# Ending a layer in two halves of rows, and beginning the next layer's sums with the first half

## The chip, the cores and the metric

The kernel runs on one core of one Trainium2 chip. The metric is the device time of one execution in microseconds, from start to end on that core. The core has a matrix engine (TensorE, "PE" in the profile), a vector engine (VectorE, "DVE"), an activation engine (ScalarE, "ACT"), a general engine (GpSimd, "POOL") and a queue engine (SyncE, "SP") that here issues most of the DMA transfers. All inputs are in HBM; the host only transposes adj and three weight matrices beforehand.

## The reference

A graph has N = 2708 nodes with D = 128 features and a dense adjacency matrix adj (2708 x 2708, about 2.4% of it nonzero). Four layers follow each other, each wrapped in the same residual normalization:

```python
x = _layernorm(x + L0(x, adj))      # gelu messages of all pairs, weighted by adj; update, gelu, layer norm
x = _layernorm(x + L1(x, adj))      # messages gated by sigmoid(q k^T) * adj * adj; update, relu, layer norm
x = _layernorm(x + L2(x, adj))      # hyperbolic attention over all pairs, expmap/logmap, relu
x = _layernorm(x + L3(x, adj))      # two sums over neighbours:

def L3(x, adj):
    neigh1 = adj @ x
    x1 = swish(neigh1 @ W + b)
    neigh2 = adj @ x1
    return swish(neigh2 @ W + b)
```

Each row of a layer's result needs every row of the input, since adj is dense in layout: `adj @ x` sums over all nodes. The sum itself may be taken in any order of nodes.

## The kernel before, in words

The 2708 rows lie in 22 row tiles of 128 rows (NT = 22, the last one has 20). x stays in SBUF as a tile of 128 partitions x 22 x 128. `runs()` cuts the row tiles into two halves, 0 to 10 and 11 to 21, and HT = 11 is the same cut.

**The order of the work.** A scheduler orders the instructions of each engine in most of the program; inside `tc.manual_schedule()` they stay in the order in which they are written. Engines take their instructions in that order, one after the other, and wait for each other by semaphores. Every DMA of adj tiles is issued by SP, in order as well.

**The ends of layers 0 and 1.** The class `Resnorm` does a layer norm of the layer's result h, the multiplication by its weight, the addition to x, and the layer norm of the sum. `normalize` takes the row moments of a run of tiles (`st`), makes a scale and an offset per row from them by a dozen small DVE instructions and one square root on ACT, and then shifts tile after tile, the even ones on DVE and the odd ones on ACT. `add(a, b)` normalizes h, multiplies and adds for a whole half at once, and takes the moments of x; `end(a, b)` normalizes x. In layer 0 the order is: add of the early half, the update of the last row tiles (`U.sums`, `U.rows`), add of the late half, end of the early half, end of the late half, then a few small operations that count rows with a problem (`bad`, `bad_n`). In layer 1 `Resnorm.all()` does the same without anything in between. Layer 1 begins with transposes of x and products with it, in groups of four row tiles; layer 2 begins with transposes of x and the products M.

**Layer 2's end.** The generator `end(hf)` does a half of the rows: transposes, then elementwise work in steps, with a `yield` after each. DVE works over 11 row tiles in each step, by `each` (one instruction per row tile), by `total` (a reduction) or by a chain of `Values` on 128 x 11 elements; ACT squares, takes square roots, tanh and logarithms. The last step normalizes x. A loop takes a step of end(1) (tiles 11 to 21), a step of end(0), and so on in turns:

```python
ends = [end(1), end(0)]
while ends:
    for e in list(ends):
        try:
            next(e)
```

**Layer 3.** `neighbours` keeps the whole transposed sum (128 x 2708) in six PSUM banks and adds adj tile after adj tile to it: for row tile j, x[:, j, :] is the stationary operand and the j-th 128 rows of adjT (1354 KB) stream past it, in six matmuls of up to 512 columns. HELD = 10 of the 22 adj tiles (0 to 9) are fetched ahead and kept for both passes; the other twelve come through three buffers in SBUF (STREAM = 3), whose pool is opened after the memory of layer 2's end is given back. `in_turns` mixes kept ("h") and streamed ("f") tiles. The second pass takes x1, made of the first pass's sums, in the same way, and after it rows are normalized and written out.

Of the kernel before, what the change touches and what calls it, by code (L numbers as in the profile page):

```python
# [20 lines left out]
P = 128  # L21
# [18 lines left out]
def gnn_stack(ctx: ExitStack, tc: tile.TileContext, t, out: bass.AP):  # L40
# [26 lines left out]
    @functools.cache  # L67
    def across(name):
        n = t[name].shape[0]
        r = const.tile([P, n], F32, name=f"row_{name}")  # L70
        nc.gpsimd.dma_start(out=r, in_=t[name].partition_broadcast(P))
        return r

# [27 lines left out]
    class Values:  # L101
# [33 lines left out]
        def add(self, a, b):  # L135
            return self.tt(a, b, ALU.add)
# [61 lines left out]

    def normalize(dst, src, st, a, b, V, sq=None):

        even, odd, m2, m5 = (st[:, a:b, k] for k in (1, 4, 2, 5))

        def stt(in0, scalar, in1, op0, op1):
            o = V.new(in0)
            nc.vector.scalar_tensor_tensor(o, in0, scalar, in1, op0=op0, op1=op1)
            return o


        d = V.tt(even, odd, ALU.subtract)
        q = stt(d, 1.0 / 16.0, d, ALU.mult, ALU.mult)  # L210
        if sq is None:
            m = stt(m2, LN_EPS * D, m5, ALU.add, ALU.add)
            w = stt(m, 0.25 / D, q, ALU.mult, ALU.add)
        else:
            m = V.tt(m2, m5, ALU.add)
            var = stt(m, 0.25 / D, q, ALU.mult, ALU.add)
            w = V.ts(var, 0.25 * LN_EPS, ALU.add)

        root = V.act(w, AF.Sqrt)
        both = V.tt(even, odd, ALU.add)  # L220
        r = V.recip(V.add(root, V.mul(w, V.recip(root))))
        off = stt(both, -0.5, r, ALU.mult, ALU.mult)
        if sq is not None:
            nc.vector.scalar_tensor_tensor(sq[:, a:b], var, 4.0 * D, V.mul(r, r), op0=ALU.mult, op1=ALU.mult)
        for i in range(a, b):
            c = slice(i - a, i - a + 1)
            if i % 2:
                nc.scalar.activation(dst[:, i, :], src[:, i, :], AF.Identity, bias=off[:, c], scale=r[:, c])  # L228
            else:
                nc.vector.tensor_scalar(dst[:, i, :], src[:, i, :], r[:, c], off[:, c], op0=ALU.mult, op1=ALU.add)  # L230

    class Resnorm:
# [4 lines left out]

        def add(self, a, b):
            h = self.h
            normalize(h, h, self.st, a, b, self.V)  # L240
            nc.vector.tensor_tensor(h[:, a:b, :], h[:, a:b, :], over_tiles(self.g, b - a), op=ALU.mult)
            nc.vector.tensor_tensor(x[:, a:b, :], self.xb[:, a:b, :], h[:, a:b, :], op=ALU.add)
            moments(self.st2, x, a, b)

        def end(self, a, b):
            normalize(x, x, self.st2, a, b, self.V, self.sq)

        def all(self):
            for a, b in runs():
                self.add(a, b)  # L250
            for a, b in runs():
                self.end(a, b)
# [124 lines left out]
    with ExitStack() as l0:  # L377
# [10 lines left out]
        with ExitStack() as msg:  # L388
# [449 lines left out]
            with tc.manual_schedule():  # L838
# [46 lines left out]
                early, late = runs()  # L885
                U.norm.add(*early)
                for n in range(ahead, G):
                    U.sums(n)
                for n in range(ahead, G):
                    U.rows(n)  # L890
                U.norm.add(*late)
                U.norm.end(*early)
                U.norm.end(*late)

# [10 lines left out]
                ps = p_misc.tile([P, BANK // P, P], F32, name="ps")  # L905
                nc.tensor.matmul(ps[:1, 0, :1], ones, most, start=True, stop=True)
                nc.vector.tensor_copy(bad_n, ps[:1, 0, :1])
# [68 lines left out]
    def layers_1_to_3(top, before_end=lambda: None):  # L976

        with ExitStack() as l1:
# [9 lines left out]
            w_both = wp.tile([P, 2 * D], F32, name="w_both")  # L988
            b_both = wp.tile([P, 2 * D], F32, name="b_both")
            xb = wp.tile([P, NT, D], F32, name="xb")  # L990
            w_msg, w_q, w_k = weight("L1_gnn_W_msg"), weight("L1_gnn_W_q"), weight("L1_gnn_W_k")
            upd_x, upd_a = weight("L1_gnn_W_upd", 0), weight("L1_gnn_W_upd", P)
            msg_bc, msg_br = column("L1_gnn_b_msg"), across("L1_gnn_b_msg")
            gate_b = across("L1_gnn_gate_bias")
            upd_b, gamma, beta = across("L1_gnn_b_upd"), across("L1_gnn_ln_gamma"), across("L1_gnn_ln_beta")

            with ExitStack() as pre:
                psum = pre.enter_context(tc.tile_pool(name="ps_pre1", bufs=2, space=PSUM))
                nc.gpsimd.memset(both[:, NT - 1, :], 0.0)
                for k, (w, b) in enumerate(((w_msg, msg_br), (upd_x, upd_b))):  # L1000
                    nc.gpsimd.tensor_copy(w_both[:, k * D:(k + 1) * D], w)
                    nc.gpsimd.tensor_copy(b_both[:, k * D:(k + 1) * D], b)
# [418 lines left out]
        HELD = min(NT, 10)  # L1421
        held = top.enter_context(tc.tile_pool(name="adj3", bufs=1))
        kept = {}
# [4 lines left out]
        with ExitStack() as fin:  # L1428
            fp = fin.enter_context(tc.tile_pool(name="fin2", bufs=1))
            tp = fin.enter_context(tc.tile_pool(name="fin2t", bufs=2))  # L1430
            psum = fin.enter_context(tc.tile_pool(name="ps_fin2", bufs=6, space=PSUM))
            VT0 = fp.tile([P, HW], F32, name="VT0")
            nc.sync.dma_start(out=VT0, in_=v_tab)
            for j in range(HELD):
                kept[j] = held.tile([P, N], F32, name=f"held{j}")
                nc.sync.dma_start(out=kept[j], in_=adjT[j * P:(j + 1) * P, :])
            u = fp.tile([P, NT, D], F32, name="u")
            sv = fp.tile([P, NT, D], F32, name="sv")
            st = fp.tile([P, NT, 6], F32, name="st")
            nc.gpsimd.memset(u[:, NT - 1, :], 0.0)  # L1440
            nc.gpsimd.memset(V0, 0.0)

            def end(hf):
                a, b = ((0, HT), (HT, NT))[hf]
                n = b - a
                V = Values(fp, f"v2{hf}_")
# [4 lines left out]
                def temp():  # L1451
                    return tp.tile([P, max(HT, NT - HT), D], F32, name="tmp")[:, :n, :]
# [76 lines left out]
            with tc.manual_schedule():  # L1529
                ends = [end(1), end(0)]  # L1530
                while ends:
                    for e in list(ends):
                        try:
                            next(e)
                        except StopIteration:
                            ends.remove(e)
        xs.close()

        with ExitStack() as l3:
            wp = l3.enter_context(tc.tile_pool(name="l3", bufs=1))
            STREAM = 3
            stream = l3.enter_context(tc.tile_pool(name="adj3s", bufs=STREAM))
            turns = l3.enter_context(tc.tile_pool(name="turns3", bufs=3))
            pacc = l3.enter_context(tc.tile_pool(name="ps_acc3", bufs=1, space=PSUM))
            psum = l3.enter_context(tc.tile_pool(name="ps_l3", bufs=2, space=PSUM))
            w3, b3 = weight("L3_gnn_W"), across("L3_gnn_b")
            V = Values(wp, "v3_")  # L1550
            nT = wp.tile([P, N], F32, name="nT")
            x1 = wp.tile([P, NT, D], F32, name="x1")
            st = wp.tile([P, NT, 6], F32, name="st")
            nc.vector.memset(x1[:, NT - 1, :], 0.0)
            banks = spans(0, N, BANK)

            def in_turns(pattern, near_by, far):

                near_by, far = list(near_by), list(far)
                order = [(near_by if c == "h" else far).pop(0) for c in pattern]  # L1560
                return order + near_by + far
# [27 lines left out]
            def neighbours(src, order, have, at_end, then, meanwhile=None):  # L1589
# [5 lines left out]
                def tile_of(j):  # L1595
                    at = have.get(j)
                    if at is None:
                        at = last[j] = stream.tile([P, N], F32, name="at")
                        nc.sync.dma_start(out=at[:rows[j], :], in_=adjT[j * P:j * P + rows[j], :])
                    return at  # L1600
# [6 lines left out]
                for j in order[:-at_end]:  # L1607
                    at = tile_of(j)
                    for k in range(len(banks)):
                        product(k, j, at)  # L1610
                    if meanwhile is not None and j == order[0]:
                        meanwhile()
# [14 lines left out]
            def finish(a, b, r, g, gate):  # L1627
# [6 lines left out]
                normalize(x, x, st, a, b, V)  # L1634
# [7 lines left out]
            far = list(range(HELD, NT))[::-1]  # L1642
            near_by = list(range(HELD))
            last = {}
            with tc.manual_schedule():
                order = in_turns("hhfhfhfhfhffhffhfffhhf", near_by, far)
                first = neighbours(x, order, kept, 3, keep)
                back = far[::-1]
                have, last = kept | {j: last[j] for j in back[:STREAM]}, {}
                order = back[:STREAM] + in_turns("hfhfhfhffhfhhhhhfff", near_by, back[STREAM:])  # L1650

                second = neighbours(x1, order, have, 6, finish, lambda: first.rows(len(banks) - 1))
                second.rows(len(banks) - 1)
# [39 lines left out]
```

## Time and profile before

| | |
|---|---|
| time, median of 3 runs | 1959.56 us (1958.17 to 1960.24) |
| the profiled execution | 1961.88 us, of which 1960.2 us are the span of the core |
| granted TensorE clock, mean over the span | 0.917 |
| PE busy | 1662.2 us (85%) |
| DVE busy | 1549.8 us (79%) |
| ACT busy | 1119.8 us (57%) |
| POOL busy | 676.7 us (35%) |
| layer 0 | from the start to about 930 us |
| layer 1 | first gate product at 958.6 us, its end 1177 to 1207 us |
| layer 2's pairs | from 1258 to 1626 us |
| layer 2's end | 1626.4 to 1715 us |
| layer 3, pass 1 and pass 2 | 1714.0 to 1830.4 us, and from there to the end |

The profile is one execution. "Busy" is the time in which an engine has an instruction at work; waits are listed apart. Times of single pieces are microseconds from the start of the span. "L1604" is line 1604 of the kernel, "x24" the number of instructions drawn together, and "<-ACT x L228" names the instruction that ended a wait, here ACT's writing x in line 228. "PEclk" is the granted TensorE clock as a share of the full one.

### The profile page before, as it was taken

Reading aid. Unit: us, or ns where it says so; the run is one execution under the profiler, and the core shown is the slowest. Engines: PE = TensorE matmul, PEld = TensorE weight load, DVE = VectorE, ACT = ScalarE, POOL = GpSimd, SP = SyncE. Lnnn points to the kernel's source line nnn. Section 1 sums busy time; section 2 is a strip of 40 time slices with the busy share of each in tenths; the row PEclk is TensorE's granted clock in tenths of the full one; section 3 lists DMA queues with packets and bytes.
Section 4 is the critical chain, followed back from the end, with each engine's and each line's share of the span. In section 5 each row is a group of like instructions: output and inputs, shape, how many; then the busy total and the mean of one; then the engine's idle time right before and its main releaser. Section 6 shows DMA issues by size and latency. Waiting matters only on the chain.

```text
span 1960.2 us, 36493 instructions
## 1 busy us (share of the span) xinstructions
PE 1662.2 (85%) x13993; PEld 952.3 (49%) x13993; DVE 1549.8 (79%) x3657; ACT 1119.8 (57%) x1551; POOL 676.7 (35%) x431
## 2 busy tenths in 40 slices
PE   5999999999999999881999992889999972099995
PEld 5666666666666666661544442322223321044542
DVE  7899999999999999868588858699999997800104
ACT  3666676676666667553344434799989973300103
POOL 5667667767767767571100000020000440000000
PEclk8899999999999999995999996889989986589997
DMA  8756667667667666440344401122222207044320
GB/s 216 162 117 146 132 129 147 127 132 149 126 132 151 121 136 141 80 88 5 131 157 159 155 3 59 45 87 87 75 69 95 97 2 298 0 160 156 135 96 30
DMA packets 218695, 222.25 MB, mean 113 GB/s; under 512 B 28373, under 2 KB 204859, under 8 KB 212051
## 3 DMA queue, kind: packets, MB, share of 16 engines
q1 hardware_dynamic: 167470, 196.15, 32.8%
q0 software_dynamic: 51040, 23.68, 10.3%
q8 instruction: 111, 1.82, 0.4%
q14 instruction: 74, 0.60, 0.1%
HBM read 211.94 MB, written 7.83 MB: 112 GB/s over the span
## 4 chain that ended last, share of the span: by engine, by line
DVE 41%; PE 31%; POOL 9%; issue 7%; DMA 6%; ACT 6%; SPq 0%; DVEq 0%; ACTq 0%; POOLq 0%
PE acc L1604 10%; POOL far L739 8%; PE lg L1063 5%; PE acc L1070 5%; DVE ix L735 5%; DMA far<-d_tab,ix 3%; DVE W L840 3%; DVE u L1322 3%; DVE w L1336 3%; DVE m L1325 3%; DVE extra L753 2%; DVE o L697 2%; DVE m L1339 2%; DVE m L1342 2%; PE sl L775 2%
## 5 line engine op out<-in xcount | busy, mean ns | idle before, releaser
L739 POOL DMA_INDIRECT far<-d_tab,ix x352 | 561.7, 1596 | 260.1 <-DVE W L840 112.6
L853 ACT ACTIVATE g<-sl 128x768 f32<-128x768 f32 x484 | 393.4, 813 | 258.0 <-PE sl L780 201.9
L775 PE MATMUL sl<-dA,S 124*128 124x153 f16 x4840 | 408.9, 232 | 10.3 <-DVE W L840 7.8
L775 PEld LDWEIGHTS <-S 124*128 124x128 f16 x4840 | 331.1, 98 | 80.1 <-issue 68.4
L791 PE MATMUL acc<-g,W 128*32 128x128 f32 x4840 | 206.1, 278 | 0.5 <-DVE W L840 0.5
L1296 POOL TENSOR_TENSOR at<-at,off 128x128 f32<-128x128 f32 (+1 forms) x22 | 68.3, 3120 | 339.9 <-DVE m L1325 171.7
L791 PEld LDWEIGHTS acc<-g,W 128*32 128x32 f32 x4840 | 140.9, 109 | 58.8 <-issue 54.8
L1604 PE MATMUL acc<-held,x 128*128 128x512 f32 (+1 forms) x240 | 99.3, 562 | 82.6 <-ACT x L228 82.6
L780 PE MATMUL sl<-s,same 50*128 50x384 f16 x968 | 162.0, 308 | 0.0
L280 DVE TENSOR_TENSOR g<-ps,row_L_gnn_b 128x512 f32<-128x512 f32 (+2 forms) x14 | 7.9, 574 | 191.5 <-PE ps L278 191.5
L840 DVE TENSOR_TENSOR W<-sl,own 128x150 f32<-128x150 f32 x484 | 143.2, 300 | 14.9 <-ACT g L853 14.7
L1352 PE MATMUL accV<-m,X 128*128 128x512 f32 (+4 forms) x264 | 130.5, 637 | 27.4 <-DVE m L1342 26.5
L1304 PE MATMUL ps<-XT 128*128 128x512 f32 (+4 forms) x264 | 142.4, 622 | 6.4 <-DVE m L1307 3.3
L1064 ACT ACTIVATE w<-lg,row_L_gnn_gate_bias 128x512 f32<-128x512 f32 (+1 forms) x132 | 83.5, 636 | 106.1 <-PE lg L1063 104.8
L665 DVE TENSOR_SCALAR S<-rk 124x1000 f16<-124x1000 bf16 (+1 forms) x330 | 133.2, 429 | 0.0
L735 DVE FIND_INDEX8 ix<-v,o 128x8 uint32<-128x2728 f32 x44 | 131.7, 2994 | 0.0
L1063 PE MATMUL lg<-qT,mT 128*128 128x512 f32 (+2 forms) x264 | 121.2, 547 | 3.6 <-ACT w L1064 3.1
L1070 PE MATMUL acc<-w,both 128*128 128x512 f32 (+2 forms) x264 | 121.2, 547 | 0.0
L753 DVE SCALAR_TENSOR_TENSOR extra<-far,v,extra 128x128 f32<-128x128 f32 x330 | 114.9, 348 | 6.3
L1604 PE MATMUL acc<-at,x 128*128 128x512 f32 (+3 forms) x288 | 118.4, 559 | 0.0
L697 DVE SCALAR_TENSOR_TENSOR o<-ps,ar 128x496 f32<-128x496 f32 x132 | 82.5, 625 | 37.5 <-issue 22.6
L1604 PEld LDWEIGHTS acc<-held,x 128*128 128x128 f32 x240 | 45.0, 196 | 134.8 <-ACT x L228 82.9
(315 smaller groups left out, 2634.8 us busy)
## 6 DMA issues: line engine op xcount, KB each, us to landing
at<-in_adjT SPq DMA_DIRECT2D x40, 1354.0 KB
ar<-in_adj SPq DMA_DIRECT2D x105, 248.0 KB
far<-s_tab SPq DMA_DIRECT2D x44, 512.0 KB
at<-in_adjT SPq DMA_DIRECT2D x42, 448.0 KB
at<-in_adjT SPq DMA_DIRECT2D x21, 704.0 KB
at<-in_adjT SPq DMA_DIRECT2D x21, 650.0 KB
held<-in_adjT SPq DMA_DIRECT2D x10, 1354.0 KB
at<-in_adjT SPq DMA_DIRECT2D x21, 280.0 KB
```

The costliest lines, as they stand in the source:

```text
L735: nc.vector.max_index(ix, self.v[:, n * 8:n * 8 + 8], self.o.rearrange("p b j -> p (b j)"))
L739: nc.gpsimd.indirect_dma_start(out=self.far[n][:, k, :], out_offset=None, in_=d_tab[:, :], in_offset=bass.IndirectOffsetOnAxis(ap=self.ix[ ...
L753: nc.vector.scalar_tensor_tensor(self.extra, f, w, self.extra, op0=ALU.mult, op1=ALU.add)
L775: nc.tensor.matmul(group[c], self.S[h][:, n, c, :], dA[q][:, b, c, :], start=c % 3 == 0 and q == 0, stop=False)
L780: nc.tensor.matmul(out, same[p], self.s3[p, :e - a, :], start=False, stop=True)
L791: nc.tensor.matmul(self.acc[q:q + 32, k, :], W[:, c, :], g[:, c, :], start=b == 0 and k == 0, stop=ends)
L840: nc.vector.tensor_tensor(W[:, :, :RG].rearrange("p (k c) i -> p k c i", k=2), columns_of(sl, D, DA), own[:, None, None, :].to_broadcast([ ...
L853: nc.scalar.activation(g.rearrange("p (k c) d -> p k c d", k=2), columns_of(sl, 0, D), AF.Gelu, scale=1.0 / D_SCALE)
L1063: nc.tensor.matmul(lg, mT[:, j * P:j * P + r], qT[:, a:b], start=True, stop=True)
L1070: nc.tensor.matmul(acc[k], mrow[:rows[j], j, :], ws[j][:rows[j], a:b], start=j == 0, stop=j == NT - 1)
L1304: nc.tensor.matmul(ps, XT[:, self.js], XT[:, c], start=True, stop=False)
L1604: nc.tensor.matmul(acc[k], src[:rows[j], j, :], at[:rows[j], a:b], start=j == order[0], stop=j == order[-1])
```

## The change

Three things change.

The ends of layers 0 and 1: `normalize` is split into `normalizer` (scale and offset) and `shift`. `Resnorm.begin` shifts a half of h wholly on ACT, `add` goes in groups of four tiles, and `all` has one order for both layers: begin and add the early half, what lies between, begin the late half, end the early half with its shifts wholly on DVE, add and end the late half. In layer 0 the small operations on `bad` now stand ahead of all this, and layer 1's joined weights and biases (`w_both`, `b_both`) are loaded side by side by DMA where POOL copied them.

The end of layer 2: end(1) is written out whole and end(0) after it; only the first step of both (transposes) still stands ahead. Temporaries, the values of end(0) and layer 3's x1 and nT are put into memory that other tiles give back.

Layer 3: one set of pools serves layer 2's end and layer 3, with two PSUM buffers beside the six sums. Seven adj tiles are kept from the beginning (11 to 15, 0 and 1), three streamed ones can be fetched ahead as well, and tiles 2 and 3 are fetched into the memory of X and of the temporaries once end(0) has read them for the last time. The first pass takes all tiles of the half 11 to 21 first.

```diff
+        def begin(self, a, b):
+            shift(self.h, self.h, a, b, normalizer(self.st, a, b, self.V), "a")
+
         def add(self, a, b):
-            h = self.h
-            normalize(h, h, self.st, a, b, self.V)
-            nc.vector.tensor_tensor(h[:, a:b, :], h[:, a:b, :], over_tiles(self.g, b - a), op=ALU.mult)
-            nc.vector.tensor_tensor(x[:, a:b, :], self.xb[:, a:b, :], h[:, a:b, :], op=ALU.add)
-            moments(self.st2, x, a, b)
-
-        def end(self, a, b):
-            normalize(x, x, self.st2, a, b, self.V, self.sq)
-
-        def all(self):
-            for a, b in runs():
-                self.add(a, b)
-            for a, b in runs():
-                self.end(a, b)
+            for k, m in spans(a, b, 4):
+                h = self.h[:, k:m, :]
+                nc.vector.tensor_tensor(h, h, over_tiles(self.g, m - k), op=ALU.mult)
+                nc.vector.tensor_tensor(x[:, k:m, :], self.xb[:, k:m, :], h, op=ALU.add)
+                moments(self.st2, x, k, m)
+
+        def end(self, a, b, turns="va"):
+            shift(x, x, a, b, normalizer(self.st2, a, b, self.V, self.sq), turns)
+
+        def all(self, between=lambda: None):
+            early, late = runs()
+            self.begin(*early)
+            self.add(*early)
+            between()
+            self.begin(*late)
+            self.end(*early, "v")
+            self.add(*late)
+            self.end(*late)
...
-                early, late = runs()
-                U.norm.add(*early)
-                for n in range(ahead, G):
-                    U.sums(n)
-                for n in range(ahead, G):
-                    U.rows(n)
-                U.norm.add(*late)
-                U.norm.end(*early)
-                U.norm.end(*late)
...
+                def between():
+                    ps = p_misc.tile([P, BANK // P, P], F32, name="ps")
+                    nc.tensor.matmul(ps[:1, 0, :1], ones, most, start=True, stop=True)
+                    for n in range(ahead, G):
+                        U.sums(n)
+                    nc.vector.tensor_copy(bad_n, ps[:1, 0, :1])
+                    for n in range(ahead, G):
+                        U.rows(n)
+
+                U.norm.all(between)
...
-                for k, (w, b) in enumerate(((w_msg, msg_br), (upd_x, upd_b))):
-                    nc.gpsimd.tensor_copy(w_both[:, k * D:(k + 1) * D], w)
-                    nc.gpsimd.tensor_copy(b_both[:, k * D:(k + 1) * D], b)
...
-        HELD = min(NT, 10)
...
-            psum = fin.enter_context(tc.tile_pool(name="ps_fin2", bufs=6, space=PSUM))
...
+        HELD, STREAM = 7, 3
+        near1 = list(range(HT, HT + 5))
+        near0 = list(range(HELD - len(near1)))
+        spare0 = list(range(len(near0), len(near0) + 2))
+        far1 = [j for j in range(HT, NT) if j not in near1][::-1]
+        far0 = list(range(spare0[-1] + 1, HT))[::-1]
...
+            turns = l3.enter_context(tc.tile_pool(name="turns3", bufs=2))
+            pacc = l3.enter_context(tc.tile_pool(name="ps_acc3", bufs=1, space=PSUM))
+            psum = l3.enter_context(tc.tile_pool(name="ps_l3", bufs=2, space=PSUM))
...
+            room = fp.tile([P, 3, HW], F32, name="room")
+            VT0, temps = room[:, 0, :], [room[:, k, :].rearrange("p (n d) -> p n d", d=D) for k in (1, 2)]
...
+            x1, nT = u, sv.rearrange("p n d -> p (n d)")[:, :N]
+            spare = dict(zip(spare0, (v.rearrange("p n d -> p (n d)")[:, :N] for v in (
+                X, room.rearrange("p k (n d) -> p (k n) d", d=D)))))
+            kept = {}
+            few = Values.within(VT1)
...
-                order = in_turns("hhfhfhfhfhffhffhfffhhf", near_by, far)
-                first = neighbours(x, order, kept, 3, keep)
-                back = far[::-1]
+                nc.sync.dma_start(out=VT0, in_=v_tab)
+                for j in near1 + near0:
+                    kept[j] = fetch(j, held.tile([P, N], F32, name=f"held{j}"))
+                ends = [end(1), end(0)]
+                for e in ends:
+                    next(e)
+                for e in ends:
+                    for _ in e:
+                        pass
+
+                def more():
+                    for j, at in spare.items():
+                        kept[j] = fetch(j, at)
+
+                order = (in_turns("fhfhfhfhfhf", h=near1, f=far1)
+                         + in_turns("hffsffsffhf", h=near0, f=far0, s=spare0))
+                assert sorted(order) == list(range(NT))
+                first = neighbours(x, order, kept, 3, keep, more, len(far1 + near1) - 1)
+                back = (far1 + far0)[::-1]
```

In the second pass the order is three streamed tiles that are still there from the first pass, then "hfhfhfhffhffhhhhfff" with the nine kept tiles as "h"; before it was "hfhfhfhffhfhhhhhfff" with ten.

## The prediction

> **What bounds the kernel now.** I read the slices of the page first, to see where TensorE (PE) is not at work; one slice is 49 us.
>
> ```profile
> span 1960.2 us, 36493 instructions
> ...
> PE   5999999999999999881999992889999972099995
> ```
>
> The digits after the last group of nines and eights, "20", are some 80 us without matmuls, between layer 2's pairs and layer 3's sums. The waits of 1626 to 1716 say for whom PE waits there:
>
> ```profile
> PE acc L1604 <- ACT x L228: 82.6, 1, 82.6
> ```
>
> One wait of 82.6 us, for the last ACT shift of layer 2's final normalization. The stretches (columns as the header names them) show what runs meanwhile, and what the first sums look like:
>
> ```profile
> core 0: us, PE busy (x) PEld busy (x) DVE busy (x) ACT busy (x) POOL busy (x), PEclk, DMA share, GB/s
> ...
> 1640.00:1660.00 20.00, 0.00 (x0) 0.00 (x0) 17.71 (x65) 8.80 (x11) 0.00 (x0) 0.50 0.95 403
> 1660.00:1680.00 20.00, 0.00 (x0) 0.00 (x0) 16.68 (x47) 8.32 (x7) 0.00 (x0) 0.50 0.00 1
> 1680.00:1700.00 20.00, 0.00 (x0) 0.00 (x0) 17.82 (x90) 7.48 (x10) 0.00 (x0) 0.50 0.00 0
> ...
> 1714.00:1726.00 12.00, 11.96 (x26) 5.52 (x27) 1.23 (x6) 1.47 (x4) 0.00 (x0) 0.82 0.66 249
> 1726.00:1738.00 12.00, 12.00 (x24) 5.18 (x23) 0.00 (x0) 0.00 (x0) 0.00 (x0) 0.72 0.32 116
> 1738.00:1770.00 32.00, 32.00 (x88) 15.26 (x87) 0.00 (x0) 0.00 (x0) 0.00 (x0) 1.00 0.36 131
> ```
>
> DVE is busy 17.7, 16.7 and 17.8 us of each 20: the stretch is bound by DVE, with ACT short and hidden. The DMA fetches the kept adj tiles at 403 GB/s until about 1659 and then idles. From 1714 PE is full, first at a granted clock of 0.82 and 0.72, then 1.00. The reader should see that no later engine is waited for: PE's first pass runs 1714.04 to 1830.4 without a pause, so whatever lets it start earlier moves the end. The times of the pieces, from PE's timeline (x12 is two matmuls for each of six banks, one adj tile):
>
> ```profile
> 1714.04 11.40 PE L1604 MATMUL acc<-held,x 128*128 128x512 f32 x24 [82.65 <-ACT x L228]
> ...
> 1738.11 4.71 PE L1604 MATMUL acc<-at,x 128*128 128x512 f32 x12
> 1742.65 4.71 PE L1604 MATMUL acc<-held,x 128*128 128x512 f32 x12
> ```
>
> Warm, a tile takes 4.54 us from start to start (1738.11 to 1742.65). The first four took 1738.11 - 1714.04 = 24.07 us, where 4 x 4.54 = 18.16: waking up cost 5.9 us.
>
> **Part D, layer 2's end and layer 3.** Removed: the interleaving of end(1) and end(0) step by step. In the new order DVE does all of end(1) (tiles 11 to 21), then all of end(0), and PE's order has eleven tiles 11 to 21 ahead of the others. What half a stretch costs I built from DVE's timeline, where each half's steps stand as blocks. The costliest row is this one, eleven row tiles in 2.98 us, and it stands once for each half:
>
> ```profile
> 1635.43 2.98 DVE L1457 SCALAR_TENSOR_TENSOR u<-X,v,u 128x128 f32<-128x128 f32 x11
> ```
>
> One half alone, each term from its own rows: product, reduction, first pass 6.67 (1631.65 to 1638.32); the square it then waits for on ACT 1.55 (1.38 and handover; before, the other half covered it); norm of it 3.56 with 0.3 waiting for the tanh (its table load, 1.28, lies beside DVE's small ones); next pass 3.8 and 0.85 of square not covered; next 6.5 and 0.65; two reductions and their norm 4.55; the chain of small 0.17 to 0.24 us instructions of one half 5.5 and 0.35 for its tanh; last pass and row moments 6.15; normalizer and shifts, up to the last ACT shift, 4.5. Sum 44.9 us. Before, both halves took 1631.65 to 1713.94, 82.3 us: half is 41.15, so 3.75 of it is ACT that is no longer covered.
>
> The first step stands ahead of both halves and has two psum buffers where it had six: PE's transposes then wait for ACT's copies. I add 1.8 (from none, if the copies keep up, to 4, if each of the six goes one after the other at 0.6). VT0's fetch is the first in SP's queue and waits for DVE and ACT by the new queue order; before it was issued at 1616.76, ahead of the end of the pairs, and landing at 430 GB/s takes under 2 us. If its memory comes free only at 1626, it costs 2 us more, for V0's copies of the other half stand ahead of end(1) on DVE.
>
> So end(1) is done at 1631.65 + 1.8 + 44.9 = 1678.35, and PE starts at 1678.4 instead of 1714.04: -35.6 us. Its first matmul takes tile 21, whose shift is the last, so nothing is gained earlier than that.
>
> What is to hold so that all of it reaches the end:
> - End(0) takes 44.9 us on, to 1723. PE's eleven tiles take 11 x 4.54 + 5.9 = 55.8 us, to 1734. 11 us of slack; the 7 us that the sequence costs over the interleaved halves (1723 against 1715) is under PE.
> - Adj tiles. At 1678 seven kept ones and three of the stream are in SBUF: 10 x 1.354 MB, as before by 1659. Fetches of tiles 18, 17, 16 wait for the stream's buffers, i.e. for PE; each needs about 3.4 us at 403 GB/s and has two turns, 9 us. Then SP's queue holds the fetches into X and into the room of the temporaries; they wait for DVE (X's last reading by end(0) about 1699, the temporaries' about 1702). They stand behind tile 16's fetch, issued about 1707, and ahead of tiles 10, 9, 8, whose buffers come free with tiles 18, 17, 16 at about 1716, 1725, 1734. Nobody waits for them before 1739. In pass 1 the stream carries 13 tiles for 12, in pass 2 ten for nine: 1.354 MB in 110 us, against 116 to 249 GB/s used of 403. I cost it at nothing; cover gone, one late tile costs up to 3.4 us.
> - x1 and nT now lie in u and sv, last read by end(0): done 1723, first written by ACT in the last three tiles of pass 1, not before 1780. Two buffers of "turns" for three: DVE takes them in order anyway. Nothing.
> - ACT loads 11 tables in these ends for 10, 1.28 us each in the trace. The rule that speaks against splitting is of the Trainium skill, ScalarE: Activation LUTs, section "What ACT_TABLE_LOAD costs": a switch is 1.28 us and a drain of 1.38, 2.66 in all, and alone a half has less work to cover it. By the rows (a load of 1.28, the function 0.01 to 0.02 after) the tanh of the norm is late by 0.3; by the rule by 1.7, and the sum would be -34.2 for -35.6. I take the row.
>
> PE is idle 45 us ahead of its start, for 82 before, so it wakes up once in both: same 5.9 us. The rule of TensorE: Matmul & The Clock Gate, "Part 1: The HAM clock gate", is half clock after some 3.4 us idle and full clock after 3.4 us busy, so 1.7 us lost; the stretches above show 0.82 and 0.72 for 24 us, and 5.9. It speaks against the change only if PE pauses between the halves: then a second wake-up, 1.7 by the rule, 5.9 by the row. I keep 5.9 for the rival.
>
> **Part A, layer 0's end** (L0 done at 897.8; layer 1's first products from 931.76).
>
> ```profile
> 931.76 1.91 PE L1019 MATMUL ps<-ident,x 128*128 128x128 f32 x8
> ...
> 942.18 1.04 PE L1019 MATMUL ps<-ident,x 128*128 128x128 f32 x8
> ...
> 958.61 1.98 PE L1063 MATMUL lg<-qT,mT 128*128 128x512 f32 x4 [0.27 <-DVE qT L1026]
> ```
>
> Six small "bad" operations go from 928.5 to ahead of the first normalizer: 1.04 us. Early shifts are all on ACT (eleven for five), at the pace of this row, 0.40 each:
>
> ```profile
> 913.50 2.41 ACT L228 ACTIVATE o<-o,g 128x128 f32<-128x128 f32 x6 [1.17 <-DVE g L205]
> ```
>
> The additions follow in groups of four, so most of that overlaps: late normalizer 2.0 later, done about 915.5. Then ACT has eleven shifts of the late half, 4.45 us, and the square root of the early half's end stands behind them; DVE waits about 4 us for it, and the late half's products behind DVE. Then eleven early shifts on DVE (0.27 each): early x ready about 924.6, and layer 1's first pair of groups, 942.18 - 931.76 = 10.4 us of PE, DVE and ACT, starts 7 us earlier, beside the late half. Price: the late half's additions stand on DVE between copies that wait for PE, so late x is ready about 939.8 for 929.6. The second pair starts about 938 instead of 942.18, and the rest follows it at its old pace: -4 us at the first gate product (958.61 before). Bounds: -8, if late x is ready as the first pair ends, and +2, if the waits of DVE for ACT and for PE add up. The four POOL copies of weights (0.28 each) that go, and the DMAs in their place at the start, are off the path; so are both.
>
> **Part C, layer 1's end**, same order. Before: early x 1201.7, late x 1207.2, moments of M, which start layer 2's chain of scalars, done 1212.6. After: early x about 1198; the late half's square root stands again behind ACT's shifts, its x is ready about 1210.5, and 19 of the 22 moments of M stand behind it on DVE: +2 us (-1, all of the early half's gain kept, to +5, ACT's 4.45 in full).
>
> **Sum.** -35.6 - 4 + 2 = -37.6. The profiled execution took 1961.88 (span 1960.2 and 1.7 around it), so 1924.3; it stands 2.3 above the median of the runs, 1959.56. Against the median: 1922.
>
> **The rivals.**
> (1) The second half is late: end(0) slowed, or X's and the room's fetches back up SP. For: 11 us of slack, and SP serves in order. Against: blocks of the trace, and DMA at 30 to 60% of its rate. Price: a pause of 4 to 8 and a second wake-up of 5.9, so 10 to 14 less gain: 1932 to 1936. It decides from 11 us of delay of end(0).
> (2) The small parts go the other way: A +2, C +5, and D -30 with VT0 late and ACT uncovered: -23, 1936. Or A -8, C -1, D -38: -47, 1913.
> (3) Slower: the first sums wait for both halves after all, one semaphore serving both. Then PE starts at 1723 plus what is uncovered, +9 against 1714, with A and C -2: +7, 1966. Against it: in the changed order PE has a wait for DVE and ACT at tile 21 and a second one for DVE before tile 0, the first of the other half. It decides where the first matmul's wait is for a shift of end(0). This is also the case that the change doesn't do what it says.
>
> **Numbers.** Forecast with its own variation (D -30 to -38, A and C within bounds) 0.80; rival 1 0.10; rival 2's slow end 0.05; rival 3 and unseen costs 0.05 (a fifth of it within 4 us). Range 1909 to 1937: it takes in both ends of rival 2 and rival 1. 0.2% is 4 us, about what a measurement can tell: faster 0.95, within 0.01, slower 0.04.
>
> **To be seen after.** One PE wait of about 45 us ends near 1676 (layers 0 and 1 take 2 off), first L3 matmul on a stream tile; 11 tiles in 56 us, then no pause at the first tile of the other half; DVE busy 45 us after PE's start; SP's fetch into X about 26 us after PE's start; early x of layer 0 ready about 925 and first gate product about 954.6. Wrong would be: PE starting past 1695, a granted clock under 0.7 beyond the first 24 us, or a pause of over 2 us behind the eleventh tile.

## The result, and the profile after

The changed kernel takes 1923.9 us (median of 4 runs, 1923.19 to 1925.2) for 1959.6 before: a ratio of 0.9813, 95% interval 0.9802 to 0.9825. The profiled execution took 1925.2 us, with a span of 1923.4, a granted clock of 0.927 and PE busy for 87%. The forecast was 1922, between 1909 and 1937.

The page, first the span and then PE's busy tenths in 40 slices (of 48 us now). Ahead of layer 3 the tenths were "720"; now they are "71", with full slices on both sides.

```profile
span 1923.4 us, 36518 instructions
...
PE   5899999999999999985699994689999997199995
```

The waits of PE over the last 330 us. The one ahead of layer 3 is 44.8 us long where it was 82.6, and it ends with an ACT shift of end(1), not of end(0):

```profile
PE acc L1613 <- ACT x L244: 44.8, 1, 44.8
```

PE's first sums (timeline: start, duration, and what), each line one adj tile of twelve matmuls, and at the foot the tiles on both sides of the border between the halves, 1734.01 being tile 0:

```profile
1676.19 9.36 PE L1613 MATMUL acc<-at,x 20*128 20x512 f32 x12 [44.83 <-ACT x L244]
1685.48 7.80 PE L1613 MATMUL acc<-held,x 128*128 128x512 f32 x12
1693.12 4.71 PE L1613 MATMUL acc<-at,x 128*128 128x512 f32 x12
...
1729.46 4.71 PE L1613 MATMUL acc<-at,x 128*128 128x512 f32 x12
1734.01 4.71 PE L1613 MATMUL acc<-held,x 128*128 128x512 f32 x12
```

There is no gap at the border, since end(0) was long done: DVE's timeline shows the same 2.98 us for eleven row tiles as before, and the last shifts of end(0) at 1717.07, of which ACT's end at 1719.1.

```profile
1635.40 2.98 DVE L1493 SCALAR_TENSOR_TENSOR u<-X,v,u 128x128 f32<-128x128 f32 x11
...
1717.07 1.63 DVE L246 TENSOR_SCALAR x<-x,VT 128x128 f32<-128x128 f32 x6
```

In stretches, DVE works beside PE until end(0) is through. What the reader should look at is PEclk: 0.50 in the first 12 us, where before had 0.82 and then 0.72.

```profile
core 0: us, PE busy (x) PEld busy (x) DVE busy (x) ACT busy (x) POOL busy (x), PEclk, DMA share, GB/s
1676.00:1688.00 12.00, 11.81 (x15) 5.00 (x16) 9.79 (x30) 3.17 (x5) 0.00 (x0) 0.50 0.13 39
1688.00:1700.00 12.00, 12.00 (x28) 5.47 (x27) 10.36 (x32) 4.25 (x4) 0.00 (x0) 0.85 0.27 102
1700.00:1734.00 34.00, 34.00 (x91) 16.06 (x90) 16.74 (x81) 7.79 (x13) 0.00 (x0) 1.00 0.59 236
```

Layer 0's end. PE's timeline around the second pair of groups of layer 1's beginning, and the stretches there:

```profile
937.25 1.40 PE L1038 MATMUL ps<-ident,x 128*128 128x128 f32 x5 [3.67 <-DVE x L246]
939.75 2.07 PE L1041 MATMUL ps_m<-xT,w_both 128*128 128x512 f32 x2 [1.11 <-ACT xT L1039]
941.62 1.91 PE L1050 MATMUL ps_w<-w_both,xT 128*128 128x256 f32 x4
...
956.80 1.98 PE L1082 MATMUL lg<-qT,mT 128*128 128x512 f32 x4 [0.27 <-DVE qT L1045]
```

```profile
937.00:946.00 9.00, 7.64 (x19) 4.63 (x20) 2.91 (x8) 3.87 (x9) 6.13 (x1) 0.62 0.00 0
946.00:956.80 10.80, 9.97 (x41) 6.11 (x40) 5.62 (x11) 2.95 (x7) 0.00 (x0) 1.00 0.00 0
```

Set side by side at six places that both traces have, the changes of the profiled executions add up (us from the start; the last column is what was gained or lost since the line above):

| place | before | after | difference | of this part |
|---|---|---|---|---|
| layer 1's first gate product | 958.61 | 956.80 | -1.81 | -1.8 |
| layer 2's first product of X | 1228.60 | 1229.43 | +0.83 | +2.6 |
| end of layer 2's pairs (first copy of VT) | 1622.78 | 1623.48 | +0.70 | -0.1 |
| layer 3's first matmul | 1714.04 | 1676.19 | -37.85 | -38.55 |
| first matmul of pass 2 | 1825.2 | 1789.33 | -35.9 | +1.95 |
| end of the span | 1960.2 | 1923.4 | -36.8 | -0.9 |

Pass 2 of the kernel before begins at 1825.2; the 1830.4 of the table before and of the prediction is one tile too late. The gain is made in one place, ahead of layer 3. 2.6 us of it were given away at the end of layer 1 and about 2 in the first two tiles of layer 3.

### The profile page after: what moved, and what is told of

It is laid out like the page before. It is cut to its first block, busy times and chain, and to the rows that moved or that the text cites. A ratio compares the mean times of both kernels' runs of the same rounds, so it can differ in the third digit from the quotient of the medians.

```text
span 1923.4 us, 36518 instructions
## 1 busy us (share of the span) xinstructions
PE 1667.8 (87%) x13993; PEld 954.2 (50%) x13993; DVE 1548.8 (81%) x3660; ACT 1125.4 (59%) x1564; POOL 677.7 (35%) x427
## 5 line engine op out<-in xcount | busy, mean ns | idle before, releaser
L1613 PE MATMUL acc<-at,x 128*128 128x512 f32 (+2 forms) x156 | 66.2, 574 | 44.8 <-ACT x L244 44.8
L1084 DVE TENSOR_TENSOR w<-w,at 128x512 f32<-128x512 f32 (+1 forms) x132 | 82.5, 625 | 26.1 <-ACT w L1083 26.1
L1371 PEld LDWEIGHTS accV<-m,X 128*128 128x128 f32 (+1 forms) x264 | 52.7, 213 | 91.7 <-issue 58.0
```

What stands on the lines that cost most here:

```text
L1371: nc.tensor.matmul(accV[:, a:b], X[:self.r, self.j, :], self.m[:, a:b], start=first, stop=last)
L1613: nc.tensor.matmul(acc[k], src[:rows[j], j, :], at[:rows[j], a:b], start=j == order[0], stop=j == order[-1])
```

## The experiments

The runs went in four groups, each on one chip beside its own runs of the kernel before (medians 1960.0, 1961.8, 1961.45 and 1960.2), so ratios to before are compared.

**The end of layer 2 and layer 3 alone.** Layers 0 and 1 end as before.

```diff
-                U.norm.all(between)
+                U.norm.add(*early)
...
+                U.norm.add(*late)
+                U.norm.end(*early)
+                U.norm.end(*late)
```

> Before with only the end of layer 2 and layer 3 changed; layers 0 and 1 end as before. Theory: the trace of after shows the two early parts to be +0.8 us together at layer 2's first product (-1.8 at the first gate product, +2.6 after it), so this kernel takes 0.8 us less than after, 1923 us, PE's first sums begin near 1675.4, and layer 0 and 1 show the landmarks of before (first gate product 958.6). Rival, the prediction's sum: the early parts are worth -2 us, so this takes 1926 us.

1923.92 us, ratio 0.9809 (0.9796 to 0.9822), PE's first sums at 1675.56. The whole gain is here, within 1 us of the changed kernel; the two early parts are together worth nothing.

**The ends of layers 0 and 1 alone**, the opposite; the diff is against before:

```diff
-                U.norm.add(*early)
...
-                U.norm.end(*late)
+                U.norm.all(between)
...
+            w_both, b_both = side_by_side()
```

> Before with only the new ends of layers 0 and 1 and the weights side by side. Theory: first gate product 956.8 (-1.8), first product of layer 2 1229.4 (+0.8), and the time 1960.4, not to be told from before. Rival, the prediction's sum: -2 us, 1957.6. Third: layers 0 and 1 are the source of most of the gain, then it lies under 1940.

1962.21 us, ratio 1.0011 (1.0003 to 1.0020): 2 us slower than before, slightly more than expected. The gate product comes at 957.20 (-1.4) and the first product of layer 2 at 1230.61 (+2.0). The sign of the prediction's sum for these two parts was wrong.

**Layer 1's end as before, the rest as changed**, to tell the two apart:

```diff
-                    norm.all()
+                    norm.all_as_before()     # add(early), add(late), end(early), end(late), whole halves, shifts "va"
```

> After, but layer 1's end in the order of before; layer 0's end stays new. Theory: the new order costs 2.6 us there, because the late half's square root stands behind eleven shifts on ACT: first product of layer 2 at 1226.8 (after 1229.4), time 1921.3 for after's 1923.9. Rival, the new order of layer 1 is neutral and the +2.6 is variation between executions: 1924 and 1229.4.

1921.24 us, ratio 0.9796 (0.9783 to 0.9809). PE's timeline at layer 2's first product, in this kernel and then in the changed one:

```profile
1226.80 2.04 PE L1333 MATMUL ps<-XT 128*128 128x512 f32 x2 [0.24 <-ACT X L1254]
```

```profile
1229.43 2.04 PE L1323 MATMUL ps<-XT 128*128 128x512 f32 x2 [0.25 <-ACT X L1244]
```

Both gate products lie within 0.13 us of each other (956.93 and 956.80), so layer 1's new end costs 2.8 us here, and layer 0's new end is worth some 2 us of what is left: by the ratios, 0.9809 to 0.9796. The intervals of these ratios overlap; that the sizes are right rests on the landmarks of the traces. DVE's timeline in the changed kernel names the wait:

```profile
1191.78 0.23 DVE L160 RECIPROCAL v<-v 128x11 f32<-128x11 f32 x1 [3.64 <-ACT v L155]
```

DVE stands 3.64 us for a square root that on ACT comes after eleven shifts. It is the root of the early half; for that of the late half, which the expectation names, DVE waits 0.20 us in this trace.

**Steps in turns.** The changed kernel with end(1) and end(0) step by step in turns again. The halves share two temporaries here, so that a half's squares are overwritten by the other's; the number of operations is the same, and only the time is read.

```diff
-                for e in ends:
-                    next(e)
-                for e in ends:
-                    for _ in e:
-                        pass
+                while ends:
+                    for e in list(ends):
+                        try:
+                            next(e)
+                        except StopIteration:
+                            ends.remove(e)
```

> After, but the steps of end(1) and end(0) in turns as before; memory, kept tiles and the order of layer 3's sums stay new. Theory: the sequence alone lets PE begin early, so PE begins where the interleaved end(1) is done, 1712 to 1714, and the time is 1958 to 1962. Rival, the gain is of the new tiles and pools (fetches ahead, other order): PE begins at 1712 but layer 3 is shorter, time under 1950.

1962.28 us, ratio 1.0010 (1.0001 to 1.0019). PE waits as long as before:

```profile
PE acc L1613 <- ACT VT L155: 82.4, 1, 82.4
```

It begins at 1715.78, 1.8 us past the latest that was expected. The kept tiles, the fetches ahead and the order of layer 3 bring nothing without the sequence.

**The first sum waits for both halves.** Sequence and all else as changed, but one tile of the other half comes first.

```diff
-                order = (in_turns("fhfhfhfhfhf", h=near1, f=far1)
-                         + in_turns("hffsffsffhf", h=near0, f=far0, s=spare0))
+                order = (near0[:1] + in_turns("fhfhfhfhfhf", h=near1, f=far1)
+                         + in_turns("ffsffsffhf", h=near0[1:], f=far0, s=spare0))
```

> After, but the first adj tile of the first pass is tile 0, whose rows of x come out of end(0); everything else in after's order. Theory: all 43 us of the lead go, since PE waits for the second half: PE begins near 1719 (end(0)'s last shift 1719.1 in after), the time is 1924 + 43 = 1967, 7 us over before, which is the price of the sequence without overlap. Rival, the lead is worth less because later waits for tiles take it back: under 1955.

1961.64 us, ratio 1.0009 (1.0000 to 1.0019): the lead is lost, as the theory says, but it is 5 us less slow than it said. Its timeline:

```profile
1716.97 7.09 PE L1613 MATMUL acc<-held,x 128*128 128x512 f32 x12 [86.20 <-DVE x L246]
1723.99 5.02 PE L1613 MATMUL acc<-at,x 20*128 20x512 f32 x12
1728.94 6.25 PE L1613 MATMUL acc<-held,x 128*128 128x512 f32 x12
```

PE begins at 1716.97, 2 us ahead of what was expected, for tile 0 is shifted by DVE at the head of end(0)'s shifts. And the first three tiles (two full, one with 20 rows, the second) cost 4.4 us over three warm ones, where the changed kernel pays 7.85. The 20-row tile is no longer first. That is the next question.

**The 20-row tile.** In the changed kernel the first tile is tile 21, whose matmuls use 20 of 128 rows. It takes 9.29 us (1676.19 to 1685.48), double the warm 4.54, and the next tile 7.64. In before it was third, and took 6.29. Theory: at 20 rows PE doesn't wake up. Three kernels tried it.

First, it is put into seventh place, where PE is long awake:

```diff
+        far1 = far1[1:4] + far1[:1] + far1[4:]
```

A second line of the edit keeps tile 21 the last streamed one in pass 2, as it was.

> After, but the 20-row tile is the seventh of pass 1 instead of the first. Theory: a first wake-up of 2.3 us, then PE at full clock, then the clock falls at the 20-row tile and the tile and its successor cost 1.75 + 1.9 more, as the third and fourth in before did: wake-up and fall together 5.9, 2 us less than after, 1922. Rival, the 20-row tile has no part in it: one wake-up of 6 to 8 us at the start and no fall at the seventh tile.

1921.28 us, ratio 0.9798 (0.9783 to 0.9813).

```profile
1673.81 7.82 PE L1614 MATMUL acc<-at,x 128*128 128x512 f32 x12 [43.82 <-DVE x L246]
1681.46 4.71 PE L1614 MATMUL acc<-held,x 128*128 128x512 f32 x12
...
1704.27 6.51 PE L1614 MATMUL acc<-at,x 20*128 20x512 f32 x12
1710.71 6.46 PE L1614 MATMUL acc<-held,x 128*128 128x512 f32 x12
1717.00 4.71 PE L1614 MATMUL acc<-at,x 128*128 128x512 f32 x12
```

The first tile is full and takes 7.65, the second 4.55. The seventh, with 20 rows, takes 6.44 (1704.27 to 1710.71) and the full one behind it 6.29, the rest 4.55 again: in the midst of busy matmuls the clock falls. The stretch of these two tiles has a granted clock of 0.74, those ahead of it and behind it 1.00:

```profile
1704.00:1717.00 13.00, 13.00 (x27) 5.76 (x26) 11.78 (x62) 4.43 (x9) 0.00 (x0) 0.74 0.87 345
```

PE's wait is 1 us shorter as well (43.82 for 44.83): it ends with a DVE shift, for the tile that comes first is no longer the one that is shifted last.

Second, the same matmuls in the first place, but over all 128 rows, of which 108 are zeros (in pass 1 alone, where x is the source):

```diff
+                def r_of(j):
+                    return P if src is x else rows[j]
...
+                        if r_of(j) > rows[j]:
+                            nc.gpsimd.memset(at, 0.0)
...
-                    nc.tensor.matmul(acc[k], src[:rows[j], j, :], at[:rows[j], a:b], ...)
+                    nc.tensor.matmul(acc[k], src[:r_of(j), j, :], at[:r_of(j), a:b], ...)
```

> After, but in pass 1 the 20-row tile's matmuls take all 128 rows (the other 108 rows of the adj tile are set to zero ahead of its fetch); order, number and width of the matmuls are the same. Theory, PE's clock looks at how many rows a matmul uses: the first tile then takes 6.9 to 7.7 us for 9.29 and the second 4.54 for 7.64, the wake-up is 2.3 to 3.1 for 7.85, the time 1919. Rival A, it looks at values that change, and zeros do nothing: no difference, 1924. Rival B, the place is what counts, the first tile pays whatever it is: 7.85 stays.

1916.81 us, ratio 0.9774 (0.9761 to 0.9787), below the interval of the changed kernel.

```profile
1676.63 7.30 PE L1619 MATMUL acc<-at,x 128*128 128x512 f32 x12 [44.84 <-ACT x L244]
1683.77 4.71 PE L1619 MATMUL acc<-held,x 128*128 128x512 f32 x12
```

7.14 for 9.29 and 4.55 for 7.64: the wake-up costs 2.6 us for 7.85. Place, number and width of the matmuls are the same, only the rows differ, so it is the rows that count; that they hold zeros does no harm.

Third, tile 21 kept and among the last three tiles of pass 1 and the last six of pass 2:

```diff
-        near1 = list(range(HT, HT + 5))
+        near1 = list(range(HT, HT + 4)) + [NT - 1]
...
+                         + in_turns("hffsffsffhzf", h=near0, f=far0, s=spare0, z=near1[4:]))
```

> After, but the row tile of 20 rows (tile 21) is a kept one and stands among the last three of pass 1 and the last six of pass 2; a full tile is the first. Theory: matmuls with 20 rows do not wake up PE's clock: in after the first tile (20 rows) takes 9.29 us and the next 7.64, a wake-up cost of 7.85; in before the clock rises by the second full tile and falls again at the 20-row tile, third. With full tiles first the wake-up costs 2.3 us (before's first two tiles: 11.34 for 9.08), so this is 5.5 us faster than after: 1918.4. Rival, the wake-up's length is a matter of when it begins: no difference beyond 2 us, 1922 to 1926.

1921.81 us, ratio 0.9793 (0.9779 to 0.9806). The first tile takes 6.82 (wake-up 2.28, as expected) and pass 1 109.5 us for 113.1, but only some 2 to 4 of the 5.5 us arrive (span and ratio): pass 1 gains 3.6 and pass 2 is 1.4 longer. Why it is longer is not shown; tile 21 stands fourth from the last there, where the changed kernel has it last.

**PE kept awake.** The changed kernel with 20 matmuls more, whose result nobody uses, while PE waits:

```diff
                 nc.vector.tensor_relu(uh, svh)
+                if hf == 1:
+                    warm = psum.tile([P, BANK], F32, name="ps")
+                    for k in range(20):
+                        nc.tensor.matmul(warm, ident, <512 columns of uh>, start=True, stop=True)
```

> After, with 20 matmuls of 512 columns more, on layer 2's values and into a spare PSUM tile whose result nobody uses, issued when end(1)'s relu is done (about 1654.5) and done by about 1675, so that PE comes to layer 3's first tile awake. Theory: the wake-up of 7.85 us falls to under 3 (the 20-row tile may still let the clock fall), time 1919 to 1921. Rival, the extra matmuls overrun the end of end(1): PE begins later by what they overrun, and 1924 or more.

1921.24 us, ratio 0.9798 (0.9784 to 0.9811). The extra matmuls, two records each, and the first tile behind them:

```profile
1654.85 20.45 PE L1547 MATMUL ps<-u,ident 128*128 128x512 f32 x40 [23.38 <-DVE v L139]
1676.33 7.67 PE L1618 MATMUL acc<-at,x 20*128 20x512 f32 x12 [1.03 <-issue]
```

They end in time (1675.3), PE begins at 1676.33; but the 20-row tile takes 7.60 even so and the next 6.80. The wake-up fell to 5.3, not under 3: the clock falls again within the first tile (0.82 from 1676.3 to 1679, 0.50 in the 5 us behind). In seventh place the 20-row tile and its follower cost 3.65 us; whether the 1.7 us more come of the pause of 1.03 us ahead of it was not tried. The expectation had left the fall open in a bracket and was too hopeful.

The intervals of three of these kernels (the 20-row tile seventh, last, and PE kept awake) overlap that of the changed kernel, 0.9802 to 0.9825. What is said of them rests on their traces; the kernel filled up with zeros is the one that is faster in time as well.

**Together.** Layer 0's end new, layer 1's as before, tile 21 kept and in the very last place of both passes; and the same with the 20 extra matmuls:

```diff
-                    norm.all()
+                    norm.all_as_before()
...
+                         + in_turns("hffsffsffhfz", h=near0, f=far0, s=spare0, z=near1[4:]))
```

> Both lessons together: layer 0's new end, layer 1's end in the order of before, and the 20-row tile kept and in the very last place of both passes. Theory: layer1_end_as_before (0.9796 of before) less 7.85 - 2.28 = 5.6 us of wake-up, plus about 1 for six changes between 128 and 20 rows in the last group: 0.9773 of before. Rival, the effects don't add, since the last group's handovers to ACT take it back: 0.979.

> best_order with the 20 matmuls ahead of layer 3's first tile (results unused). Theory: the first tile is now full and PE is awake, so the wake-up of 2.3 us falls to under 0.3: 2 us less than best_order, 0.9763 of before. Rival, the gap of about 1 us between the extra matmuls and the first tile, or their end, costs as much as it saves: as best_order.

1917.37 us, ratio 0.9776 (0.9763 to 0.9790), and 1913.06 us, ratio 0.9754 (0.9741 to 0.9768). All five runs of the second are below all five of the first, which went beside them. In the second the first tiles run at full speed from the start:

```profile
1672.49 4.78 PE L1628 MATMUL acc<-at,x 128*128 128x512 f32 x12
1677.11 4.71 PE L1628 MATMUL acc<-held,x 128*128 128x512 f32 x12
```

Finally tile 21 is filled up with zeros as well:

```diff
+                    if rows[j] < P:
+                        nc.gpsimd.memset(at, 0.0)
                     kept[j] = fetch(j, at)
-                    nc.tensor.matmul(acc[k], src[:rows[j], j, :], at[:rows[j], a:b], ...)
+                    nc.tensor.matmul(acc[k], src[:, j, :], at[:, a:b], ...)
```

> best_order_awake, but the kept tile 21 is filled up with rows of zeros and all its matmuls take 128 rows, in both passes. Theory: the handovers between 128 and 20 rows in the last groups cost best_order 0.1 to 0.2 us each, about 2 us in both passes, and go: 0.9745 of before, pass 1 under 106 us from PE's start. Rival, the last groups are bound by ACT's copies of the sums, so nothing is gained there: 0.9754 as best_order_awake.

1910.47 us (1908.88 to 1912.18), ratio 0.9745 (0.9732 to 0.9758); pass 1 takes 105.4 us. This is the fastest kernel of the study, 13 us faster than the changed one. Its interval and that of the one ahead of it overlap, so the last step alone is likely, not shown; in the profiled executions pass 1 takes 105.4 us for 107.2, and the time from the first matmul of pass 2 to the end 131.5 for 133.9.

## Why the prediction was right, point by point

- **Where the gain lies.** It was to come from DVE's stretch of 82 us before layer 3, and did. Steps in turns gives the whole of it back, the end of layer 2 alone has the whole of it.
- **The sum of one half, 44.9 us.** Measured from 1631.61 to the last shift at 1676.1: 44.5. The waits for ACT that lost their cover were put at 1.55, 0.3, 0.85, 0.65 and 0.35; DVE's timeline has 1.50, none beyond the 0.28 of the square root, 0.87, 0.50 and none. The rule of the Trainium skill, ScalarE: Activation LUTs, "What ACT_TABLE_LOAD costs", with 2.66 us for a switch would have put 1.4 more on the tanh; the trace of after has 1.28 for the load and the function 0.02 us behind it. The measurement agrees with the row.
- **The first step, +1.8.** The prediction gives no reason for this term, and it was wrong: the step cost nothing. PE's first eight transposes now run from 1624.33, ahead of the last copies of the pairs' sums, and DVE has V0 at 1631.61, as before, although the pairs ended 0.7 later. The term is -0.75 where it was +1.8; with 0.4 from the half's sum it makes the -38.55 out of the -35.6. That PE's wait ended at 1676.19, where "near 1676" was forecast, is luck: layers 0 and 1 took 0.7 us more, where 2 less were expected, and this term hid it.
- **Cover for what was costed at nothing.** End(0) was to take 44.9 and end at 1723; it was done at 1719.1, 15 us ahead of tile 0, not 11. The price of the sequence, put at 7 us (8 by its own 1723 and 1715), was 5: 1719.1 for 1713.94. The fetches into X and the room went at 1707.4 and 1707.8, the tiles were used at 1747.6 and 1761.3; no wait for a DMA is seen in pass 1. Rivals 1 and 3 did not come about. The run that forces rival 3 is slower than before by 0 to 3.7 us, not by 7: end(0)'s first tile came 2 us earlier and the wake-up was 3.4 shorter.
- **The wake-up, "same 5.9 us".** This step failed. I had taken the wake-up as a thing that is paid once and is the same, and did not look at which tile pays it. The four first tiles of before were 2 full ones (2.26 over two warm ones) and then the 20-row one (1.75) with its follower (1.9). So what I read as one slow wake-up was a short one and a fall. With the 20-row tile first it became 7.85, +1.95.
- **Layer 0's end, -4.** Less than half of it came, -1.8. Early x, late x (shifts until 939.1) and the second pair's start (937.25) were as worked out. The step that failed is "the rest follows it at its old pace": PE stands still for 3.67 us before that pair, as the line above shows, and works on at a clock of 0.62 until 946, where the same work of before, without that gap, had 1.00 (its row stands below). The kernel with layer 1's end as before has the same gap, 3.67 us, and the same clock, 0.62. The rule of TensorE: Matmul & The Clock Gate, "Part 1: The HAM clock gate", that some 3.4 us without work put PE to half clock, agrees with this row. I had weighed it for layer 3 only, where there is one gap in both kernels, and not for the place where the change makes a new one, though my own figures had it: a first pair done by 935.2 and a second from 938. And the second pair's copies of x stand on ACT behind six shifts: PE waits 1.11 us for them, 0.24 before. From the second pair's start to the gate product it is 19.55 us for 16.43; of these 3.1 us some 0.9 are the copies', the rest lies in matmuls at the lower clock. No run takes the gap alone away.

```profile
942.00:951.00 9.00, 8.76 (x36) 5.54 (x35) 4.37 (x7) 2.45 (x4) 0.00 (x0) 1.00 0.01 2
```

- **Layer 1's end, +2.** It is +2.6 to +2.8, by the mechanism named, a square root behind ACT's shifts: the late half's, eleven in this row,

```profile
1187.31 4.34 ACT L244 ACTIVATE both<-both,v,v 128x128 f32<-128x128 f32 x11 [1.16 <-DVE v L216]
```

  and the early half's root behind them. The prediction named the late half's root here, which is wrong; early x and late x, put at 1198 and 1210.5, came at 1196.0 and 1209.0, or 1197.8 and 1210.8 with the 1.8 us that layer 0 had gained. It was rightly put down as a loss, in a change that was not made for one.
- **The sum** was -37.6 for the profiled execution and is -36.7. Errors of -2.95 in the stretch, +1.95 in the wake-up, +2.2 in layer 0's and +0.6 in layer 1's end, and -0.9 at the end of pass 2 nearly cancel. The mechanism was right; that the number came out within 2 us is in part luck.

## What to carry to other kernels

When an elementwise stage stands between two stages of matmuls and the matmuls add up over rows, finish half of the rows first: the pipeline costs a few microseconds of uncovered waits on the other engines and gives back the time of the other half, as long as the matmuls of the first half outlast it. Where such an edit opens new gaps on PE, look which matmuls come first behind each gap: a gap of 3.7 us took back about half of what the overlap at layer 0's end was to bring. Put full tiles first, fill a ragged tile up with zeros, and keep a shift whose result is not urgent from standing ahead of a small operation that another engine waits for.

## What was not expected of the hardware

Matmuls with 20 rows did not raise PE's clock, and let it fall, as a pause does. A tile of twelve matmuls with 20 rows takes 9.29 us as the first one, runs PE down from 4.54 to 6.44 us a tile in the midst of full ones, and makes its follower slow (6.29); with 108 rows of zeros added it takes 7.14 as the first, 2.6 over a warm one. For full tiles first, without matmuls ahead of them, the wake-up was 2.3 to 3.1 us, which is half clock for some 4.5 to 6.3. By the rule of TensorE: Matmul & The Clock Gate, "Part 1: The HAM clock gate" (full clock after at least one busy window of about 3.4 us), 1.7 would be the least, an estimate; since the window there runs freely and does not begin with the work, the runs do not contradict it. That the number of rows matters, it does not tell. Which number of rows is enough, between 20 and 128, was not tried.
